# Layer 3 of a graph network: 30 blocks by count matrices instead of 29, own rows on VectorE, the shared row split once, dense products spread to the last fetches

## The chip, the cores and the metric

The kernel runs on one core of a Trainium2 chip. The time is device microseconds (us) of one execution. The kernel before took 2103.5 us, the median of three runs (2099.63 to 2105.44).

## The reference

Three graph-convolution layers over 6250 nodes and 100000 edges, a residual and a layer norm. The edges arrive sorted by destination.

```
src, dst = edges + one loop per node;  deg = count of dst;  dinv = 1/sqrt(deg)
h = x                                              # 6250 x 256
for W, b in ((W1, b1), (W2, b2), (W3, b3)):        # widths 512, 512, 256
    h = relu(segment_sum((h @ W)[src] * dinv[src] * dinv[dst], dst) + b)
out = layernorm(x + h)
```

## The kernel before

**Blocks and tables.** The 6250 nodes are 50 blocks of Q = 125. Each layer has a table in DRAM, one row per node, already multiplied by dinv of its source; the aggregation of a block sums the rows of all sources of its edges, adds the block's own rows (the loops), and multiplies by dinv of the destination. In layer 3 the product with W3 has been taken before (in the work that closes layer 2's blocks), so layer 3 is aggregation, bias, relu, residual and layer norm alone. Every fp32 value is split into a high part and a rest (both float32r, a faster format of TensorE), side by side in 512 columns: `parts` holds so the split rows of all nodes in SBUF, and one 512-column product sums both halves.

**Two ways to aggregate a block.** *Gathered:* GpSimd fetches 128 rows of the table at a time by an indirect DMA (`gather`, L1172); ScalarE casts the high half (L1232), VectorE subtracts for the rest (L1235), and TensorE multiplies by a 0/1 matrix that says to which of the 125 destinations a row belongs (L1200). Such a fetch is a *chunk*; a block has KF = 16. Edges beyond 2048 of a block share one more fetch per ten blocks, the *shared row tile*; in layer 3 it isn't split, so its product is a plain fp32 one (half as many columns, recorded as two matmuls). The 0/1 matrices are made four at a time by VectorE (`more_hots`, L1123), when the first of four is needed. The block's own rows come in by a product with the identity, first in its sum (L1185). *Dense:* a 125 x 6250 matrix of uint8 counts says how often each node is a source; five 125x125 pieces at a time are converted to float32r by ScalarE, every fourth by VectorE (L1132), and 50 products of such a piece with `parts` make the block's sum (L1269). The loops are added into the count matrix (L813).

**Who does what.** `MANY` = 29 blocks (0 to 28) of layer 3 are dense and 21 gathered. Their count matrices are made before: 26 in layer 1, and the others in layer 2, at chunks 50 + gap x n with gap = (612 - 100) // (MANY - 26) = 170. Making one takes 25 bf16 products (L862), 15 comparisons on VectorE (L787), 13 copies out of PSUM on ScalarE (L821), one addition (L813), and a store to DRAM on SP's queue. Layer 2 itself has 38 gathered blocks (608 chunks) and 12 dense ones that TensorE works on beside them.

**Order.** Inside `layer` the instructions of all engines are put out by hand in one loop over chunks (L1217): gather chunk c, cast chunk c-3, subtract chunk c-4, products of chunk c-lag (lag = 9 in layer 3), then the steps of the work that closes finished blocks (`after3`), then dense products until `done` reaches begun + (c + 1 - first) x 50 / spacing (L1249). 45 dense products of block 0 have been done before (`begun`). For layer 3 spacing = (339 - 14) / (29 - 0.9), 339 being the chunks of 21 blocks and three shared tiles; from the last chunk on all dense products that are left are put out at once (L1252). Each engine runs its own list in order and waits on semaphores.

**Closing a block** (`after3`, L1432): load its rows of x on SP's queue (two buffers), sum x dinv + bias and the second half (L1438, L1439), relu and add x (L1444), statistics (L1447, L1449), square root on ScalarE (L1451), reciprocal and scaling (L1454, L1455), store on ScalarE's queue.

Of the kernel before, what the change touches and what calls it, by code (L numbers as in the profile page):

```python
# [10 lines left out]
F32 = mybir.dt.float32  # L11
# [5 lines left out]
ALU = mybir.AluOpType  # L17
# [9 lines left out]
Q = 125  # L27
# [7 lines left out]
HOTS = 4  # L35
# [3 lines left out]
LOANED = 4  # L39
RETURN = 6  # L40
SHORT = 5


COPIED = 3
# [6 lines left out]
BOTH_FROM = 26  # L51
# [4 lines left out]
SPLIT = ((3, 4, BOTH_LAG), (1, 2, 8), (3, 4, 9))  # L56
# [1 line left out]
TEAM = 3  # L58
TEAMS = 4
HOME = 19  # L60
MANY = 29
ALONE = 2
G = 5
GB = Q // G
# [333 lines left out]
def sorted_path(ctx: ExitStack, tc: tile.TileContext, x, edges, starts, found, wts, biases, room, late, out):  # L398
# [14 lines left out]
    nc = tc.nc  # L413
# [4 lines left out]
    N, C = x.shape  # L418
    HID = w1_sb.shape[2]
    EC = d.shape[1]  # L420
    NB = N // Q
# [11 lines left out]
    parts = all_parts[:Q]  # L433
# [3 lines left out]
    dinv = const.tile([Q, NB], F32, name="sdinv")  # L437
# [301 lines left out]
    work = ctx.enter_context(tc.tile_pool(name="swork", bufs=2))  # L739
# [12 lines left out]
    split = split_rows_of(one, "sfirst_split", 0, C)  # L752
# [251 lines left out]
    begun = 0  # L1004
# [36 lines left out]
    def layer(i, width, gathered, dense, after, rows, first=0, spacing=1.0, extras=(), filler=None):  # L1041
# [19 lines left out]
        total = len(items)  # L1061
# [53 lines left out]
        hots = []  # L1115
# [21 lines left out]
        hi_lag, lo_lag, lag = SPLIT[i]  # L1137
# [9 lines left out]
        acc = own_product = None  # L1147

        of_ten, to_split = {}, {}
        ten_halves = split.popleft() if i == 1 else None  # L1150
        shared, rows = rows[:2], rows[2:]

        def gather(c):
            nonlocal turn
            n, b, j = items[c]
            table = both_halves if of_both(c) else tables[i]
            if (i, b, j) == (0, BOTH_FROM, BOTH_LAG + 1):
                hot_stores.appendleft(late_hot_room)
            if b is None:
                row, at = split.popleft() if of_both(c) else shared[n % 2], rest[:, n, 0:1]  # L1160
                of_ten[n] = row
                if i == 1:
                    to_split[c + SPLIT[i][2] + 1] = n
            elif of_both(c):
                row, at = split.popleft(), src[:, b, j:j + 1]
                split_rows[c] = row
            else:
                row, at = rows[turn % len(rows)], src[:, b, j:j + 1]
                assert i > 0 or b < TAIL_FROM or len(hot_stores) == 2
                (landed if halved(c) else split_rows)[c] = row  # L1170
                turn += 1
            nc.gpsimd.indirect_dma_start(out=row, out_offset=None, in_=table,  # L1172
                                         in_offset=bass.IndirectOffsetOnAxis(ap=at, axis=0))

        def product(c):
            nonlocal acc, own_product
            n, b, j = items[c]
            if b is None:
                return
            if j == 0:  # L1180
                acc = sum_bank("acc", 2 if i == 1 else 3)
                own_product = i == 2 or i == 0 and b < BOTH_FROM
                if own_product:

                    nc.tensor.matmul(acc[:Q], lhsT=ident_r[:Q, :Q], rhs=parts[:, b], start=True, stop=False)  # L1185
            if i == 1 and j == KF - LATE:
                by_rows(nc.sync, own_row, tables[1][b * Q:(b + 1) * Q, :])
            several = [(j, split_rows.pop(c))]
            if j == KF - 1:
                several.append((KF, of_ten[b // GRP]))  # L1190
            for k, row in several:
                at = n * (KF + 1) + k
                if at % HOTS == 0:
                    more_hots()
                hot = hots[at // HOTS][:, at % HOTS]
                if row.dtype != F32R:
                    hot = hot.bitcast(F32)
                size = min(row.shape[1], HID)
                for c0 in range(0, row.shape[1], size):
                    nc.tensor.matmul(acc[:Q, :size], lhsT=hot, rhs=row[:, c0:c0 + size], start=(not own_product and k == c0 == 0),  # L1200
                                     stop=(k == KF and c0 + size == row.shape[1]))
            halves = several[0][1]
            if i == 1 and halves in loaned:
                on_loan.remove(halves)
            if halves.dtype == F32R and (returning is None or halves not in loaned):
                split.append(halves)
            if j == KF - 1:
                if i == 1:
                    nc.scalar.activation(own_row, own_row, AF.Copy, scale=dinv[:, b:b + 1])
                ended(now, b, acc)  # L1210
# [3 lines left out]
        with tc.manual_schedule():  # L1214
            more_hots()
            to_sum = 0
            for chunk in range(total + (SHORT if i == 1 else lag)):  # L1217
                now = chunk
                if i == 1:
                    lag = SPLIT[i][2] if returning is None else max(SHORT, SPLIT[i][2] - (chunk - returning) // 2)  # L1220
                if i == 0:
                    lag = TAIL_LAG if TAIL_FROM * KF <= chunk - total + NB * KF < (NB - 1) * KF else BOTH_LAG
# [26 lines left out]
                until = min(len(dense) * NB, begun + int((chunk + 1 - first) * NB / spacing))  # L1249
                if i == 0:  # L1250
                    until = min(until, done + 3)
                if chunk >= total - 1:  # L1252
                    until = len(dense) * NB
                while done < until:
                    m, k = divmod(done, NB)
# [176 lines left out]
    def after3(b, acc, bank):  # L1432
        yield from take("y", 2)
        x_rows.reverse()
        xr = x_rows[0]
        by_rows(nc.sync, xr, x[b * Q:(b + 1) * Q, :])
        y = work.tile([Q, HID], F32, name="szs")[:, :C]
        nc.vector.scalar_tensor_tensor(y, acc[:Q, :C], dinv[:, b:b + 1], b3_sb[:Q], op0=ALU.mult, op1=ALU.add)  # L1438
        nc.vector.scalar_tensor_tensor(y, acc[:Q, C:], dinv[:, b:b + 1], y, op0=ALU.mult, op1=ALU.add)  # L1439
        free(bank, acc)  # L1440
        yield LATE
        r_o = work.tile([Q, HID], F32, name="st")
        r, o = r_o[:, :C], r_o[:, C:]
        nc.vector.scalar_tensor_tensor(r, y, 0.0, xr, op0=ALU.max, op1=ALU.add)  # L1444
        yield 1
        stats = small.tile([Q, nc.vector.BN_STATS_DIM], F32, name="sstats")
        nc.vector.bn_stats(stats, r)  # L1447
        mv = small.tile([Q, nc.vector.BN_AGGR_DIM], F32, name="smv")
        nc.vector.bn_aggr(mv, stats)  # L1449
        sd = small.tile([Q, 1], F32, name="ssd")  # L1450
        nc.scalar.activation(sd, mv[:, 1:2], AF.Sqrt, bias=eps[:Q])  # L1451
        yield SOON
        rs = small.tile([Q, 1], F32, name="srs")
        nc.vector.reciprocal(rs, sd)  # L1454
        nc.vector.tensor_scalar(o, r, mv[:, 0:1], rs, op0=ALU.subtract, op1=ALU.mult)  # L1455
        free("y")
        by_rows(nc.scalar, o, out[b * Q:(b + 1) * Q, :], store=True)
# [12 lines left out]
    def steps(b):  # L1470

        return (NB - b) * KF + NG - b // GRP
# [13 lines left out]
    spacing = 15.0  # L1486
# [26 lines left out]
    nc.sync.dma_start(out=b3_sb, in_=bass.AP(tensor=b3.tensor, offset=b3.offset, ap=[[0, P], [1, C]]))  # L1513
    pieces = ctx.enter_context(tc.tile_pool(name="slate_pieces", bufs=6))
    split = split_rows_of(ctx, "ssplit", 2, C)
    spacing = (steps(MANY) - 14) / (MANY - begun / NB)
    layer(2, C, every[MANY:], many, after3, last_rows, 4, spacing)


# [179 lines left out]
```

## Time and profile before

| | |
|---|---|
| median of three runs | 2103.5 us |
| profiled execution | 2099.5 us, its span 2097.8 us |
| TensorE clock granted, mean | 0.961 |
| layer 2's first gather, layer 3's first gather | 708.5 us, 1646.5 us |
| layer 3's last gather, end | 2084.4 us, 2097.8 us |
| busy in the span | PE 93%, DVE 74%, ACT 64%, POOL 68% |

PE is TensorE's matmuls, PEld its weight loads, DVE VectorE, ACT ScalarE, POOL GpSimd, SP the sync engine; a q behind a name is that engine's instruction queue issuing transfers. The slices cut the span in 40 equal parts, each digit a busy share in tenths. In a group of instructions stand line, engine, operation, what is written and read with the shape, the count, then busy us and mean ns of one, then the idle time just before them and who ended it. Matmuls are pipelined and overlap in the record, so busy time of PE says that something was on it, not how fast it went.

### The profile page before, as it was taken

The page shows a single profiled execution, that of the slowest core. Times are in us where ns is not written, and L with a number is a line of the kernel's source. Part 1 is how long each engine was busy: PE and PEld are TensorE (multiplying, and loading weights), DVE is VectorE, ACT ScalarE, POOL GpSimd, SP SyncE. Part 2 cuts the span into 40 slices and gives each one's busy share as a digit, 9 for nine tenths or more (in the row PEclk, how much of TensorE's full clock was granted, in tenths as well). Part 3 has the DMA queues.
Part 4 walks back from the last instruction along what each step waited for, and adds up shares of the span by engine and source line. Part 5 has one row for each costly group of instructions (what it writes and reads, how often), then busy time and mean ns, then how long its engine had stood idle before and what let it go on. Part 6 is the DMA issues. An engine that isn't in the chain of part 4 may idle for free.

```text
span 2097.8 us, 30169 instructions
## 1 busy us (share of the span) xinstructions
PE 1944.3 (93%) x8687; PEld 1513.0 (72%) x8687; DVE 1555.1 (74%) x2933; ACT 1351.9 (64%) x2584; POOL 1432.8 (68%) x1442
## 2 busy tenths in 40 slices
PE   3489999999998979999999999999998899999996
PEld 2367777777775656788778877887777688888874
DVE  5866778787777668877787777778786377777777
ACT  1566777777776667777776766667665456555553
POOL 2456766777676477767776677577776477777775
PEclk6599999999998989999999999999999999999998
DMA  7877999999999899989998999899978376767674
GB/s 167 260 241 209 256 242 249 248 254 256 250 258 301 229 294 255 264 251 283 290 257 244 279 284 269 236 250 299 267 234 229 99 188 175 192 177 195 172 191 116
DMA packets 235407, 493.47 MB, mean 235 GB/s; under 512 B 43633, under 2 KB 85965, under 8 KB 235231
## 3 DMA queue, kind: packets, MB, share of 16 engines
q0 software_dynamic: 122112, 311.41, 54.3%
q1 hardware_dynamic: 97279, 168.19, 29.1%
q10 hardware_dynamic: 15840, 11.86, 2.3%
q8 instruction: 70, 1.15, 0.2%
q14 instruction: 106, 0.87, 0.1%
HBM read 423.84 MB, written 67.46 MB: 234 GB/s over the span
## 4 chain that ended last, share of the span: by engine, by line
PE 61%; DMA 17%; issue 8%; POOL 6%; DVE 4%; ACT 2%; ACTq 1%; SPq 0%; POOLq 0%; DVEq 0%
DMA room<-tab,ssrc 13%; PE sacc L1200 11%; PE mat_ps L1269 7%; PE smm L1269 6%; POOL room L1172 6%; PE win_ps L1269 6%; PE win_ps L1385 5%; PE sacc L1269 5%; PE str L1269 2%; PE win_ps L1405 2%; PE sacc L1322 2%; PE mat_ps L970 2%; PE sacc L970 2%; PE smm L970 2%; PE win_ps L1200 1%
## 5 line engine op out<-in xcount | busy, mean ns | idle before, releaser
L1172 POOL DMA_INDIRECT room<-tab,ssrc x1040 | 1069.2, 1028 | 398.4 <-issue 168.5
L1235 DVE TENSOR_TENSOR halves<-room,halves 128x512 fp32r<-128x512 f32 (+1 forms) x778 | 427.1, 562 | 242.3 <-ACT halves L1232 233.4
L1232 ACT CAST halves<-room 128x512 fp32r<-128x512 f32 (+1 forms) x778 | 388.9, 517 | 229.9 <-DMA room<-tab,ssrc 175.3
L1200 PE MATMUL sacc<-halves,shot 128*125 128x512 f32 x1384 | 479.4, 411 | 15.4 <-DVE shot L1123 6.6
L1172 POOL DMA_INDIRECT halves<-both,ssrc x352 | 331.0, 940 | 143.6 <-issue 36.8
L1132 ACT CAST piece<-room 125x625 fp32r<-125x625 uint8 x416 | 294.5, 717 | 84.1 <-DVE halves L1235 27.3
L787 DVE TENSOR_TENSOR room<-near_cols,slots 128x625 bf16<-128x625 f32 (+2 forms) x390 | 294.2, 801 | 44.9 <-PE sacc L862 21.3
L1200 PEld LDWEIGHTS sacc<-halves,shot 128*125 128x125 f32 x1384 | 257.3, 190 | 89.5 <-issue 9.4
L1123 DVE TENSOR_TENSOR shot<-near_cols,sdlo 128x500 fp32r<-128x500 f32 x371 | 247.4, 667 | 6.2 <-PE smm L1200 3.7
L1385 PE MATMUL win_ps<-room,w_sb 128*128 128x250 f32 (+1 forms) x832 | 189.9, 372 | 9.3 <-DVE st L1418 4.3
L1269 PE MATMUL mat_ps<-parts,piece 125*125 125x512 f32 x650 | 188.1, 406 | 0.0
L1385 PEld LDWEIGHTS win_ps<-room,w_sb 128*128 128x128 f32 x832 | 154.4, 192 | 36.3 <-DVE st L1418 6.2
L1269 PE MATMUL win_ps<-parts,piece 125*125 125x512 f32 x600 | 172.5, 409 | 5.5 <-ACT piece L1132 5.5
L1269 PE MATMUL smm<-parts,piece 125*125 125x512 f32 x605 | 172.7, 404 | 0.6 <-DVE piece L1132 0.6
L1235 DVE TENSOR_TENSOR parts<-room,parts 128x512 fp32r<-128x512 f32 x198 | 134.2, 689 | 46.8 <-ACT parts L1232 43.6
L932 DVE TENSOR_TENSOR parts<-parts 125x512 fp32r<-125x512 f32 x200 | 137.8, 689 | 30.3 <-ACT parts L930 29.8
L970 PE MATMUL sacc<-parts 125*125 125x512 f32 x400 | 141.8, 427 | 18.0 <-ACT parts L930 10.4
L1232 ACT CAST parts<-room 128x512 fp32r<-128x512 f32 x198 | 120.1, 622 | 52.5 <-DMA room<-tab,ssrc 37.1
L862 PEld LDWEIGHTS <-room 128*125 128x125 bf16 x650 | 89.8, 140 | 76.8 <-issue 30.6
L821 ACT CAST room<-sacc 125x500 uint8<-125x500 f32 (+1 forms) x152 | 105.7, 705 | 60.7 <-PE sacc L862 59.0
L1269 PE MATMUL sacc<-parts,piece 125*125 125x512 f32 x450 | 143.1, 425 | 1.6 <-ACT piece L1132 1.6
L970 PE MATMUL mat_ps<-parts 125*125 125x512 f32 x400 | 137.3, 425 | 0.3 <-DVE st L1327 0.2
(311 smaller groups left out, 3146.4 us busy)
## 6 DMA issues: line engine op xcount, KB each, us to landing
parts<-tab SPq DMA_DIRECT2D x105, 448.0 KB
kept<-room SPq DMA_DIRECT2D x29, 683.6 KB
room<-kept SPq DMA_DIRECT2D x29, 683.6 KB
room<-tab,ssrc POOLq DMA_INDIRECT x1040
tab<-st SPq DMA_DIRECT2D x62, 224.0 KB
both<-parts SPq DMA_DIRECT2D x10, 1120.0 KB
own_row<-tab SPq DMA_DIRECT2D x38, 224.0 KB
parts<-kept SPq DMA_DIRECT2D x60, 136.7 KB
```

The costliest lines, as they stand in the source:

```text
L787: nc.vector.tensor_tensor(out, near_cols[:, :shape[2]].unsqueeze(1).to_broadcast(shape), numbers.unsqueeze(2).to_broadcast(shape), op=ALU. ...
L821: nc.scalar.copy(place[:, :, u * G:(u + len(ms)) * G].rearrange("p k (t r) -> p t k r", r=G), counted_in.rearrange("p (t v) -> p t v", t=2 ...
L932: nc.vector.tensor_sub(to[:, HID:], row, to[:, :HID].bitcast(F32))
L970: nc.tensor.matmul(team_banks[n][:Q], lhsT=team_pieces[(g * CUTS + k // PIECE) % 2][n][:, k % PIECE, :], rhs=both_parts[u % 3][:, h * HID: ...
L1123: nc.vector.tensor_tensor(hot[:, :n], near_cols[:, :Q].unsqueeze(1).to_broadcast([P, n, Q]), dlo.rearrange("p b j -> p (b j)")[:, at:at + ...
L1132: convert(piece, made_or_read[:, c * PIECE:(c + 1) * PIECE, :])
L1172: nc.gpsimd.indirect_dma_start(out=row, out_offset=None, in_=table, in_offset=bass.IndirectOffsetOnAxis(ap=at, axis=0))
L1200: nc.tensor.matmul(acc[:Q, :size], lhsT=hot, rhs=row[:, c0:c0 + size], start=(not own_product and k == c0 == 0), stop=(k == KF and c0 + si ...
L1232: nc.scalar.copy(halves[:, :width], landed[chunk - hi_lag])
L1235: nc.vector.tensor_sub(halves[:, width:], landed.pop(chunk - lo_lag), halves[:, :width].bitcast(F32))
L1269: nc.tensor.matmul(acc_d[:Q], lhsT=got[done // PIECE][:, k % PIECE, :], rhs=parts[:, k], start=(k == 0), stop=(k == NB - 1))
L1385: nc.tensor.matmul(h_ps[:, f, :], lhsT=w2_sb[:, k, (f2 + f) * P:(f2 + f + 1) * P], rhs=zt2[:, k, :wide], start=(k == 0), stop=(k == KH - 1))
```

## The change

Five edits, all for layer 3 (i = 2) but the first, which also adds a matrix to layer 2's work. `MANY` goes from 29 to 30. The shared tile is split once for its ten blocks, into a tile of its own, as layer 2 does it. Own rows of a gathered block are added by VectorE in `after3`, out of `parts`. The next four 0/1 matrices are made as soon as the last product with the previous four has been put out. The lag falls from 9 to 6 over the last chunks (`AT_END`), the spacing is (322 + 1) / (30 - 0.9), and what dense products are left is put out only five chunks after the last gather.

```diff
+END = 1
+AT_END = 6
...
-MANY = 29
+MANY = 30
...
-        ten_halves = split.popleft() if i == 1 else None
+        ten_halves = split.popleft() if i > 0 else None
...
-                if i == 1:
+                if i > 0:
                     to_split[c + SPLIT[i][2] + 1] = n
...
-                own_product = i == 2 or i == 0 and b < BOTH_FROM
+                own_product = i == 0 and b < BOTH_FROM
...
-                if at % HOTS == 0:
+                if at // HOTS == len(hots):
                     more_hots()
...
+            if i == 2 and (at + 1) % HOTS == 0:
+                more_hots()
...
-            for chunk in range(total + (SHORT if i == 1 else lag)):
+            for chunk in range(total + (lag, SHORT, AT_END)[i]):
                 now = chunk
+                if i == 2:
+                    lag = max(AT_END, SPLIT[i][2] - max(0, chunk - total + 2 * AT_END) // 2)
...
-                if chunk >= total - 1:
+                if chunk >= (total + AT_END - 2 if i == 2 else total - 1):
                     until = len(dense) * NB
...
-        y = work.tile([Q, HID], F32, name="szs")[:, :C]
-        nc.vector.scalar_tensor_tensor(y, acc[:Q, :C], dinv[:, b:b + 1], b3_sb[:Q], op0=ALU.mult, op1=ALU.add)
-        nc.vector.scalar_tensor_tensor(y, acc[:Q, C:], dinv[:, b:b + 1], y, op0=ALU.mult, op1=ALU.add)
+        z = work.tile([Q, HID], F32, name="szs")
+        y, lower = z[:, :C], acc[:Q, C:]
+        if b < MANY:
+            nc.vector.scalar_tensor_tensor(y, acc[:Q, :C], dinv[:, b:b + 1], b3_sb[:Q], op0=ALU.mult, op1=ALU.add)
+        else:
+            nc.vector.tensor_tensor(z, acc[:Q], parts[:, b].bitcast(F32), op=ALU.add)
+            nc.vector.scalar_tensor_tensor(y, y, dinv[:, b:b + 1], b3_sb[:Q], op0=ALU.mult, op1=ALU.add)
+            lower = z[:, C:]
+        nc.vector.scalar_tensor_tensor(y, lower, dinv[:, b:b + 1], y, op0=ALU.mult, op1=ALU.add)
...
-    spacing = (steps(MANY) - 14) / (MANY - begun / NB)
+    spacing = (steps(MANY) + END) / (MANY - begun / NB)
     layer(2, C, every[MANY:], many, after3, last_rows, 4, spacing)
```

## Prediction

> **What bounds the kernel now.** The page comes first: engine totals, then the slices. In the slices TensorE is the engine at 9 almost throughout, and its digit falls only in the last one.
>
> ```profile
> PE 1944.3 (93%) x8687; PEld 1513.0 (72%) x8687; DVE 1555.1 (74%) x2933; ACT 1351.9 (64%) x2584; POOL 1432.8 (68%) x1442
> PE   3489999999998979999999999999998899999996
> ```
>
> Layer 3 runs from 1646 us to the end at 2097.8. The table of busy time by stage shows how it is spent:
>
> ```profile
> 1646.00:1700.00 54.00, 48.08 (x195) 37.75 (x194) 30.91 (x78) 28.18 (x62) 41.04 (x42) 0.94 0.58 153
> 1700.00:1750.00 50.00, 50.00 (x217) 40.03 (x216) 36.25 (x97) 29.09 (x68) 38.12 (x40) 1.00 0.69 186
> 2000.00:2050.00 50.00, 49.71 (x214) 39.47 (x213) 38.08 (x103) 29.78 (x71) 38.42 (x39) 1.00 0.67 178
> 2050.00:2098.00 48.00, 31.10 (x114) 21.34 (x112) 33.21 (x91) 17.38 (x45) 27.08 (x28) 0.82 0.39 113
> ```
>
> (Columns: stretch, length, busy us of PE, PEld, DVE, ACT, POOL, then clock, DMA share, GB/s.) TensorE is full until 2050 and then does 114 products in 48 us, where the stretches before did 217 in 50. That last stretch is where this change acts. The groups of layer 3, by shape, give what each engine has to do in it:
>
> ```profile
> L1172 POOL DMA_INDIRECT room<-tab,ssrc x336 | 333.0, 991 | 102.4 <-issue 32.3 <-DVE halves L1235 25.6 <-DVE piece L1132 7.3
> L1269 PE MATMUL win_ps<-parts,piece 125*125 125x512 f32 x500 | 139.9, 404 | 5.5 <-ACT piece L1132 5.5
> L1200 PE MATMUL sacc<-halves,shot 128*125 128x512 f32 x336 | 134.3, 405 | 8.7 <-DVE shot L1123 5.5 <-DVE srs L1454 1.8 <-DVE halves L1235 1.4
> L1269 PE MATMUL smm<-parts,piece 125*125 125x512 f32 x455 | 125.0, 397 | 0.6 <-DVE piece L1132 0.6
> L1269 PE MATMUL mat_ps<-parts,piece 125*125 125x512 f32 x450 | 123.6, 397 | 0.0
> L1200 PE MATMUL sacc<-room,shot 128*125 128x256 f32 x42 | 12.9, 390 | 0.0
> L1185 PE MATMUL sacc<-parts,ident_r 125*125 125x512 f32 x21 | 8.5, 403 | 0.0
> ```
>
> Dense products are 500+455+450 = 1405, products of gathered rows 336, halves of the shared row's fp32 product 42, own-row products 21. Each lasts about 0.4 us, but they overlap, so I need the distance of two starts. The order of time gives it, and the two ends of the layer:
>
> ```profile
> 1646.47 0.95 POOL L1172 DMA_INDIRECT room<-tab,rest  x1 [26.58 <-DMA tab<-st]
> 1654.64 7.54 PE L1269 MATMUL win_ps<-parts,piece 125*125 125x512 f32 x20 [5.27 <-ACT piece L1132]
> 2061.99 1.33 PE L1269 MATMUL win_ps<-parts,piece 125*125 125x512 f32 x5
> 2072.16 0.86 PE L1200 MATMUL sacc<-halves,shot 128*125 128x512 f32 x3
> 2072.86 0.59 PE L1200 MATMUL sacc<-room,shot 128*125 128x256 f32 x2
> 2081.47 2.29 PE L1200 MATMUL sacc<-halves,shot 128*125 128x512 f32 x4 [2.23 <-DVE shot L1123]
> 2084.36 0.95 POOL L1172 DMA_INDIRECT room<-tab,ssrc  x1 [0.30 <-DVE halves L1235]
> 2089.81 0.48 DVE L1438 SCALAR_TENSOR_TENSOR szs<-sacc,sdinv,sb 125x256 f32<-125x256 f32 x1 [1.54 <-PE sacc L1200]
> 2092.95 0.78 ACTq L75 DMA_DIRECT2D out<-st  x2
> ```
>
> Five products in 1.33 us, the last of them 0.4 long: (1.33-0.40)/4 = **0.232 us from start to start**. A half of the shared row's fp32 product: 0.59-0.39 = 0.20; I take 0.215, between that and 0.232. GpSimd issues 339 gathers from 1646.47 to 2084.36: 437.9/338 = **1.296 us a gather**, never waiting longer than 0.3 us:
>
> ```profile
> POOL room L1172 <- issue: 32.9, 108, 0.3
> ```
>
> So two engines are full side by side until 2072: TensorE by the products that the spacing puts between gathers, and GpSimd by issuing. At 2072.16 the dense products are done while eleven gathers are still to be issued, and TensorE then waits for each row. The products left at 2072.16 are those of block 49 and the last three of block 48: some 17 of gathered rows, two shared pairs, one own row, 17 x 0.232 + 4 x 0.215 + 0.23 = 5.0 us of work. They end at 2089.8. **TensorE loses 2089.8 - 2077.2 = 12.6 us there.** Then 8.0 us of the last block's normalisation and store follow to 2097.8.
>
> **The change part by part.** (a) *One block from gathered to dense.* 16 gathers and one shared gather go (block 29 no longer opens a group), 339 to 322. 16 products go, 50 dense ones come. Last gather issued: 1646.5 + 321 x 1.296 = 2062.4, instead of 2084.4.
>
> (b) *Shared row split once.* 42 fp32 halves go (9.0 us); 20 single products of 0.232 come (4.6 us). ScalarE and VectorE get two 128x256 operations each, while 16 casts and subtractions of that size go with block 29's rows. The second split writes the tile that block 39's last product reads; ScalarE meets it two chunks later in the order, so a wait there is short, behind it stand row casts, and TensorE has up to four converted pieces (20 products, 4.6 us) in hand. Nothing is charged.
>
> (c) *Own rows by VectorE.* 21 products go from TensorE (4.9 us), 20 additions of 125x512 out of PSUM come to VectorE. Layer 1 has that very operation:
>
> ```profile
> L1304 DVE TENSOR_TENSOR szs<-sacc,parts x9: 678/690/692, 284.2 to 698.0; 125x512 f32<-125x512 f32 x9
> ...
> L1235 DVE TENSOR_TENSOR halves<-room,halves 128x256 fp32r<-128x256 f32 x336 | 136.2, 418 | 110.3 <-ACT halves L1232 109.8
> ```
>
> The first row is one operation's median in ns (690), the second the groups' mean of one subtraction (418). 20 x 0.69 = 13.8 us on an engine that is busy 36 to 38 of 50 us; block 29's 16 subtractions of 0.42 (6.7 us) go at the same time. VectorE stays near three quarters, so the additions lie in its idle time; without that cover they cost up to 13.8.
>
> TensorE's work in layer 3: 50 x 0.232 = 11.6 added, 16 x 0.232 = 3.7, 9.0 - 4.6 = 4.4 and 4.9 removed: **1.4 us less**. The totals are nearly equal; what changes is where the idle time goes.
>
> (d) *Spacing and lag.* Dense products now run 4.5 a chunk to chunk 326 of 328, so there is always one to do between the last rows; the lag of product behind gather falls from 9 to 6 over the last chunks. TensorE per chunk: (1455+340)/322 x 0.232 = 1.293 us, against 1.296 for a gather. TensorE's end is then the full-queue end, 2077.2 - 1.4 = 2075.8. The last row is issued at 2062.4; a row needs from issue to product what the chain of waits shows at the end,
>
> ```profile
> 2084.36 2.77 DMA room<-tab,ssrc
> ```
>
> 2.77 and then a cast and a subtraction, ready at 2088.1, 3.8 us after its issue. That is 2066.2: 9.6 us ahead of TensorE. So TensorE ends the layer: **2089.8 - 2075.8 = 14.0 us earlier**. Comparison matrices (L1123) are now made one product early; waits on them such as the 2.23 us at 2081.47 should go. I credit none of it in the full stretch.
>
> (e) *The end.* Block 49 and dense block 29 finish within half a us of each other. In VectorE's order all of block 29's seven operations stand ahead of block 49's last ones. One block takes from 2089.81 to 2092.95, 3.1 us, some 2.6 of it VectorE. Block 29 starts about 0.5 us before; and the own-row addition is 0.7: 2.6 - 0.5 + 0.7 = **2.8 us longer** than the 8.0 now. (Between 0.7, if they interleave without loss, and 3.3.) The x rows of both are on time: SP loads them as soon as one of two buffers is free, and for the last blocks of before it did so from 2058 on, before their last products:
>
> ```profile
> 2058.34 16.88 SPq L77 DMA_DIRECT2D room<-in_x  x8
> ```
>
> (f) *One more count matrix in layer 2.* 25 count products, 15 comparisons on VectorE, 13 copies on ScalarE, one store and later its load on SP's queue (a whole count matrix, as for the 29 before). The four late matrices start 128 chunks apart, where three did at 170.
>
> ```profile
> L787 DVE TENSOR_TENSOR hot_pair<-near_cols,slots 128x625 bf16<-128x625 f32 (+2 forms) x36 | 27.8, 801 | 0.7 <-PE str L862 0.5
> ...
> 951.00:1047.00 96.00, 95.16 (x426) 77.66 (x425) 74.27 (x119) 68.78 (x125) 74.18 (x71) 1.00 1.02 286
> 1060.00:1185.00 125.00, 123.88 (x574) 101.42 (x573) 98.02 (x162) 90.87 (x172) 88.47 (x83) 1.00 0.93 259
> 1185.00:1299.00 114.00, 108.31 (x482) 86.55 (x481) 87.67 (x140) 78.37 (x146) 82.17 (x81) 1.00 1.03 281
> 1313.00:1438.00 125.00, 123.92 (x573) 101.33 (x572) 96.38 (x158) 88.95 (x168) 85.37 (x81) 1.00 0.93 255
> 1317.59 0.27 PE L862 MATMUL str<-hot_pair 128*125 128x250 bf16 x1
> 1317.70 0.59 PE L1385 MATMUL win_ps<-room,w_sb 128*128 128x250 f32 x2
> ```
>
> Three late matrices took 36 of these comparisons after 850 us, 0.8 us each, so a new one brings VectorE 12 us. The second and fourth stretch hold a count matrix, the others none. With one, a gather (last x column) takes 125/83 = 1.51 and 125/81 = 1.54 us, without one 1.35 and 1.41. But the count stretches also hold more products per gather (574/83 = 6.9 against 6.0), because the team's blocks finish in them, and TensorE is full: 574 products in 125 us is 0.218 each. So I charge TensorE's time alone: the next product starts 0.11 us behind a count product, 25 x 0.11 = **2.8 us**. Bounds: 0 (the matrix falls into a stretch with idle time) and 15.7, the largest difference of pace, (1.543-1.352) x 82 chunks.
>
> Sum: -14.0 + 2.8 + 2.8 = **-8.4 us**. The profiled execution took 2099.5 us around its span of 2097.8; the median of the runs is 2103.5. I subtract from the median: **2095.1**.
>
> **A rule of the skill.** The stretches show PEld at 40 of 50 us where PE is at 50. The Trainium skill, Perfetto Trace Analysis, "Identifying the Most-Contended Engine", says that matmul busy time is a bad measure and LDWEIGHTS busy share a good one: by it TensorE has a fifth to spare. The Trainium skill, TensorE: Matmul & The Clock Gate, "Wait — 56ns, not 53.3ns?", gives 215.7 ns for a warm 512-column product; at that (an estimate from the page) the 1795 products would need 387 us and not 416. The trace has 0.232 at a clock of 1.00 in group after group, and that is what I go by.
>
> **Rivals.**
> 1. *TensorE isn't the bound; it keeps up with whatever GpSimd issues.* Then the end follows the last gather: 2062.4 + 5.4 (2084.36 to 2089.8) = 2067.8, 8.0 us before 2075.8: -16.4, **2087**. For it: GpSimd is as full as TensorE. Against: products stand 0.232 apart without gaps. 8%.
> 2. *The last rows are late at lag 6.* Six chunks are 7.8 us, 3.8 are needed; VectorE, with the additions and two closing blocks, would have to add 4. Then TensorE stops for a row with dense products queued behind it, and some 5 us of the 12.6 come back: **2100**. For it: the old tail shows exactly such waits. Against: the margin of 9.6 us. 12%.
> 3. *Slower: the count matrix is paid by the pace of its stretch.* Comparisons of 0.8 us on VectorE delay subtractions, rows come free late, gathers late. At 15.7 us: -8.4 + 12.9 = +4.5, **2108**. It decides from 11.2 us upwards. For it: the pace above. Against: the extra products explain the pace. 14%.
>
> **How the numbers follow.** The forecast has 66%, with a range of its own of 2089 to 2101 (tail 0.7 to 3.3, matrix 0 to 6, waits on comparisons gone or not). Rivals 1 and 3 lie at the edges, so the range is 2086 to 2107. About 0.3%, 6.3 us, is what a measurement of this kernel can tell from no change (the three runs spread by 5.8). Faster: four fifths of the forecast and rival 1, 0.6; within: the rest of the forecast, rival 2 and most of rival 3, 0.34; slower: 0.06.
>
> **What would show it.** Right: TensorE at 9 to the last slice; the last dense and the last gathered product within 1 us of each other; the last gather some 8 us or more before them; layer 3 from first gather to last product about 429 us instead of 443; layer 2 longer by 2 to 4. Wrong: products of gathered rows that wait for VectorE or ScalarE in the last 20 us; a first gather of layer 3 later by over 8 us; or products closer than 0.23.

## The result, and the profile after

The changed kernel takes **2129.73 us** (median of 6 runs, 2123.05 to 2135.28) against 2103.81 for the kernel before on the same chip (6 runs, 2094.49 to 2106.19): ratio **1.0139, 95% interval 1.0116 to 1.0162**, slower (the two medians alone divide to 1.0123, 25.9 us). The forecast was 2095.1, faster; the time lies outside its range.

The profiled execution took 2124.5 us, its span 2122.8. The two lines of the page that answer to the first two shown of before:

```profile
PE 1942.2 (91%) x8703; PEld 1509.0 (71%) x8703; DVE 1573.8 (74%) x2953; ACT 1362.4 (64%) x2590; POOL 1418.5 (67%) x1425
PE   3499999999997879999999999989988899999997
```

TensorE has as much to do as before, in 25 us more. Behind the first three, besides the slices that were low before too (13, 15, 31 and 32), slices 14, 27 and 30 fell; the last two lie in layer 2, where only a count matrix was to be added. The last slice went from 6 to 7.

The profiled executions are divided at gathers. One of these places needs a word: the table above the prediction calls 708.5 us layer 2's first gather, but that is layer 1's last one; layer 2's 612 gathers start at 728.2 us, after an idle stretch. The lengths called "layer 2" from here on run from layer 1's last gather, in every run, and so hold some 20 us between the layers (19.7 in before, 19.9 in after); the differences are hardly touched by it.

| us | before | after | difference |
|---|---|---|---|
| layer 1, first gather to its last | 632.4 | 630.5 | -1.9 |
| layer 2, layer 1's last gather to layer 3's first | 938.0 | 972.8 | **+34.8** |
| layer 3, first gather to the end | 451.3 | 442.4 | **-8.9** |

Two executions of one kernel differ by up to 3 us in layer 2 and in layer 3 (e1 and e16, e6 and e18 below), and by up to 6 in layer 1. Layer 3 came near what was forecast (-11.2 = -14.0 + 2.8), layer 2 lost four times that. The table by stage and the order of time of layer 3 after (columns as in the prediction):

```profile
2000.00:2050.00 50.00, 50.00 (x216) 39.92 (x216) 40.06 (x104) 29.65 (x70) 38.42 (x39) 1.00 0.71 187
2050.00:2100.00 50.00, 48.20 (x206) 37.74 (x205) 41.60 (x110) 28.09 (x66) 37.03 (x37) 1.00 0.64 174
2100.00:2123.00 23.00, 11.72 (x51) 9.03 (x49) 10.80 (x30) 4.69 (x13) 0.00 (x0) 0.81 0.11 28
```

```profile
2097.05 0.95 POOL L1174 DMA_INDIRECT room<-tab,ssrc  x1 [0.30 <-DVE smv L1461]
2109.93 1.32 PE L1275 MATMUL mat_ps<-parts,piece 125*125 125x512 f32 x5
2111.09 0.64 PE L1202 MATMUL sacc<-halves,shot 128*125 128x512 f32 x2
2111.29 0.48 DVE L1446 SCALAR_TENSOR_TENSOR szs<-mat_ps,sdinv,sb 125x256 f32<-125x256 f32 x1 [4.90 <-PE mat_ps L1275]
2117.76 0.78 ACTq L77 DMA_DIRECT2D out<-st  x2
```

The last dense and the last gathered product lie 0.5 us apart, and the last gather is issued 14 us ahead of them: the picture that the prediction drew. Then the group of L1200 (now L1202), on the page of before and on that of after:

```profile
L1200 PE MATMUL sacc<-halves,shot 128*125 128x512 f32 x1384 | 479.4, 411 | 15.4 <-DVE shot L1123 6.6
```

```profile
L1202 PE MATMUL sacc<-halves,shot 128*125 128x512 f32 x1388 | 482.0, 412 | 60.7 <-DVE shot L1125 55.1
```

The idle time ahead of these products went from 15.4 to 60.7 us, and nearly all of the rise is put down to `shot`, the 0/1 matrices. Where it is, the waits of TensorE in layer 2 of after (from 850 to 1674 us) tell; the columns are us in all, how many, and the longest:

```profile
PE sacc L1202 <- DVE shot L1125: 41.0, 31, 5.3
PE win_ps L1371 <- ACT room L1402: 3.8, 5, 1.1
```

31 waits, the longest 5.3 us. In the same stage of before, 850 to 1640, the longest line and the one for `shot` are:

```profile
PE sacc L1290 <- DVE szs L1341: 4.7, 3, 3.2
PE sacc L1200 <- DVE shot L1123: 0.2, 1, 0.2
```

Over the whole kernel, and for all gathered rows, this line goes from 6.6 us in before to 68.1 in after (the group above holds only the rows in `halves`):

```profile
PE sacc L1200 <- DVE shot L1123: 6.6, 6, 2.5
```

```profile
PE sacc L1202 <- DVE shot L1125: 68.1, 54, 5.3
```

**The mechanism.** In both versions there is one more call of `more_hots()`, ahead of the loop over chunks (L1215, now L1219). I had overlooked it, and the text above the prediction says so wrongly ("when the first of four is needed"). With `at % HOTS == 0` the call at product 0 is already the second one: group 1 is made when group 0 is first used, so the matrices run a whole group, four products, ahead. With `at // HOTS == len(hots)` the call at product 0 falls away, because one group is there; group 1 is made only when product 4 asks for it. The line that makes it earlier stands under `i == 2` alone. So layers 1 and 2 lost a lead of four products, and layer 3 went from four products to one (to none for one group in seventeen, which begins at a block's shared row: the added line looks only at the last product put out). Layer 1 shows no loss by it (-1.9). The longest of the waits, in order of time, with VectorE's and ScalarE's rows that bear on it (others are left out):

```profile
1417.37 0.69 DVE L1241 TENSOR_TENSOR halves<-room,halves 128x512 fp32r<-128x512 f32 x1 [2.23 <-ACT halves L1238]
1419.76 0.62 ACT L1238 CAST parts<-room 128x512 fp32r<-128x512 f32 x1 [1.81 <-DMA room<-tab,ssrc]
1420.41 0.76 DVE L1241 TENSOR_TENSOR parts<-room,parts 128x512 fp32r<-128x512 f32 x1 [2.35 <-ACT parts L1238]
1422.23 0.69 DVE L1241 TENSOR_TENSOR parts<-room,parts 128x512 fp32r<-128x512 f32 x1 [1.05 <-ACT parts L1238]
1422.84 0.67 DVE L1125 TENSOR_TENSOR shot<-near_cols,sdlo 128x500 fp32r<-128x500 f32 x1
1423.56 1.22 PE L1202 MATMUL sacc<-halves,shot 128*125 128x512 f32 x2 [5.32 <-DVE shot L1125]
```

The comparison needs no gathered row and takes 0.67 us, yet in VectorE's list it stands behind the subtractions of rows that belong to later chunks (layer 2 subtracts two chunks behind the gather and multiplies up to eight behind it). Those wait for ScalarE, and ScalarE waits for a transfer (1.81). TensorE's product, whose own row was long split, waits for all of that: 5.32 us. In before the comparison stands in the same list, four products earlier; there such a delay is met by nobody (0.2 us).

### The profile page after: what moved, and what is told of

It is laid out like the page before. It is cut to its first block, busy times and chain, and to the rows that moved or that the text cites. A ratio compares the mean times of both kernels' runs of the same rounds, so it can differ in the third digit from the quotient of the medians.

```text
span 2122.8 us, 30261 instructions
## 1 busy us (share of the span) xinstructions
PE 1942.2 (91%) x8703; PEld 1509.0 (71%) x8703; DVE 1573.8 (74%) x2953; ACT 1362.4 (64%) x2590; POOL 1418.5 (67%) x1425
## 4 chain that ended last, share of the span: by engine, by line
PE 32%; DMA 5%; issue 4%; DVE 4%; ACT 2%; POOL 2%; SPq 1%; ACTq 0%; DVEq 0%; POOLq 0%
PE sacc L1202 8%; PE win_ps L1275 5%; PE mat_ps L1275 4%; PE win_ps L1391 4%; PE smm L1275 4%; DMA room<-tab,ssrc 3%; PE win_ps L1411 2%; POOL room L1174 2%; DMA own_row<-tab 1%; PE smm L972 1%; PE mat_ps L972 1%; PE sacc L972 1%; DVE halves L1241 1%; DVE shot L1125 1%; ACT halves L1238 1%
## 5 line engine op out<-in xcount | busy, mean ns | idle before, releaser
L1174 POOL DMA_INDIRECT room<-tab,ssrc x1024 | 1056.9, 1032 | 423.4 <-issue 157.9
L1241 DVE TENSOR_TENSOR halves<-room,halves 128x512 fp32r<-128x512 f32 (+1 forms) x762 | 421.0, 564 | 214.9 <-ACT halves L1238 207.3
L1202 PE MATMUL sacc<-halves,shot 128*125 128x512 f32 x1388 | 482.0, 412 | 60.7 <-DVE shot L1125 55.1
L1238 ACT CAST halves<-room 128x512 fp32r<-128x512 f32 (+1 forms) x762 | 382.5, 520 | 184.0 <-DMA room<-tab,ssrc 106.3
L1134 ACT CAST piece<-room 125x625 fp32r<-125x625 uint8 x423 | 299.7, 717 | 104.6 <-PE mat_ps L1275 25.1
L1202 PEld LDWEIGHTS sacc<-halves,shot 128*125 128x125 f32 x1388 | 253.6, 189 | 142.8 <-DVE shot L1125 59.5
L1275 PE MATMUL mat_ps<-parts,piece 125*125 125x512 f32 x700 | 199.8, 404 | 0.0
L1275 PEld LDWEIGHTS mat_ps<-parts,piece 125*125 125x125 f32 x700 | 125.9, 187 | 30.0 <-issue 2.3
L1202 PE MATMUL sacc<-parts,shot 128*125 128x512 f32 x396 | 131.1, 412 | 13.5 <-DVE shot L1125 13.1
```

Source lines behind the costliest of these rows:

```text
L1134: convert(piece, made_or_read[:, c * PIECE:(c + 1) * PIECE, :])
L1238: nc.scalar.copy(halves[:, :width], landed[chunk - hi_lag])
L1241: nc.vector.tensor_sub(halves[:, width:], landed.pop(chunk - lo_lag), halves[:, :width].bitcast(F32))
L1275: nc.tensor.matmul(acc_d[:Q], lhsT=got[done // PIECE][:, k % PIECE, :], rhs=parts[:, k], start=(k == 0), stop=(k == NB - 1))
```

## The experiments

Unless told otherwise they are compared with runs of before on the same chip, and "layer 2" and "layer 3" are the stages of the table above, from one profiled execution each. One thing is needed to read them: e9, e11 and c0 fell on a chip where the kernel before itself takes 2357 us, e12 to e15 on one where it takes 2333 us; their times are set only beside runs of that same chip, and times in us that were expected for them do not apply there.

### The 0/1 matrices: e1, e2, e3

e1 is the changed kernel with the old condition, and without the two added lines:

```diff
-                if at // HOTS == len(hots):
+                if at % HOTS == 0:
...
-            if i == 2 and (at + 1) % HOTS == 0:
-                more_hots()
```

> The changed kernel with one line put back: a group of four 0/1 matrices is made at every fourth product again (the first call before the loop then keeps the groups four products ahead), and the extra call of layer 3 goes. Theory A (the lost lookahead of four products is the whole loss): layer 2, first gather to first gather of layer 3, back from 973 us to 938 + 3 = 941, waits of TensorE for 0/1 matrices from about 41 us back to under 10, layer 3 about 440, time 2092 to 2099, ratio to before 0.995 to 0.998. Theory B (my rival 3: the 30th count matrix and the closer spacing of the late ones slow layer 2): layer 2 stays at 965 to 975, time 2120 to 2130.

Measured: 2099.81 us, ratio **0.9974** (0.9957 to 0.9990); again on another chip, as e16 below, 0.9987 (0.9964 to 1.0009). Layer 2 952.1 instead of 972.8. TensorE's only line for `shot`:

```profile
PE sacc L1202 <- DVE shot L1125: 1.7, 4, 0.7
```

e2 is the opposite: the kernel before with nothing but the new condition.

```diff
-                if at % HOTS == 0:
+                if at // HOTS == len(hots):
```

> The kernel before with that one line changed alone (a group is made when its first product asks for it), 29 matrices, old tail. Theory A: layer 2 grows by 30 us or more with no matrix added, layer 3 some us longer too because it has no early call here, time 2130 to 2145. Theory B: no change, 2100 to 2108.

Measured: 2136.87 us, ratio **1.0146** (1.0125 to 1.0166). Layer 2 971.0 (before 938.0), layer 3 459.1 (451.3), since here no line makes up for it in layer 3. TensorE's waits:

```profile
PE sacc L1200 <- DVE shot L1123: 76.7, 55, 6.5
```

So the condition alone costs 31 us, and taking it back out of the changed kernel gives 0.0165 of the time, 35 us (30 by the medians, which come from different chips): this is shown, from both sides.

e3 asks how much lead is needed: the changed kernel with its "one product early" in all layers.

```diff
-            if i == 2 and (at + 1) % HOTS == 0:
+            if (at + 1) % HOTS == 0:
```

> The changed kernel with the call after every fourth product in all three layers and not in layer 3 alone: lookahead one product. Theory A: the loss in layer 2 depends on how far ahead the group is made; one product of layer 2 is about 1.4 us of a chunk, against 0.67 us for the group plus what stands before it on VectorE, the longest wait being 5.7 us, so about half of the 35 us comes back: layer 2 at 950 to 960, time 2105 to 2118. Theory B: 2120 to 2130.

Measured: 2103.44 us, ratio 0.9994 (0.9970 to 1.0018), better than expected. Layer 2 949.7, as in e1. Over the whole kernel the waits fall to half only, from 68.1 us:

```profile
PE sacc L1202 <- DVE shot L1125: 36.1, 35, 3.0
```

One product of lead gives back nearly all. It also shows that a sum of waits isn't time lost: 36 us of waits here, next to none in e1, and layer 2 is the same; in the whole time e3 is 0.002 above e1, within the intervals. The longest single wait is 3.0 us here against 5.3 in after and 6.5 in e2; that the long ones are what counts fits this, but no run tests it.

### The 30th count matrix: e4, e5, e6, e9, e12, e14, e15

e4 is the kernel before, with a 30th count matrix made and stored in layer 2 and never read; unused work is added, nothing is left out.

```diff
-    kept = dram.tile([MANY, Q, NB * Q], U8, name="kept")
+    kept = dram.tile([MANY + 1, Q, NB * Q], U8, name="kept")
...
-    gap = (steps(TEAM * TEAMS) - 100) // (MANY - FEW - EXTRA)
+    gap = (steps(TEAM * TEAMS) - 100) // (MANY + 1 - FEW - EXTRA)
...
-          + [(50 + gap * n, counts([b], (made,))) for n, b in enumerate(many[FEW + EXTRA:])]
+          + [(50 + gap * n, counts([b], (made,))) for n, b in enumerate(every[FEW + EXTRA:MANY + 1])]
```

> The kernel before with a 30th count matrix made and stored in layer 2 (late ones 128 chunks apart instead of 170) and never read; all else as before. It leaves nothing out and adds unused work. Theory A: 25 x 0.11 = 2.8 us, time 2104 to 2109. Theory B: 12 to 35 us more, time 2115 to 2138.

Measured: 2111.35 us, ratio 1.0029 (1.0008 to 1.0050), 6 us; 2.8 us would be 1.0013, inside the interval. In the profile layer 2 is 949.9, 12 longer. Its two stretches from 1510 to 1530 us, while and just after the DMA engines are full, and then those of before:

```profile
1510.00:1520.00 10.00, 4.25 (x13) 1.98 (x12) 7.61 (x13) 5.36 (x10) 7.56 (x9) 0.74 1.06 289
1520.00:1530.00 10.00, 9.96 (x38) 7.93 (x39) 8.17 (x14) 7.45 (x15) 5.85 (x6) 0.74 0.98 295
```

```profile
1510.00:1520.00 10.00, 7.81 (x28) 4.84 (x27) 7.32 (x12) 6.31 (x11) 7.56 (x9) 1.00 1.04 298
1520.00:1530.00 10.00, 7.90 (x27) 6.59 (x28) 9.94 (x18) 8.18 (x15) 7.56 (x9) 0.66 0.91 286
```

In e4 the fourth store was issued at 1489 us, just ahead, and TensorE did 13 products from 1510 to 1520 instead of 28. The first stretch alone flatters the effect: in the second e4 does more than before, and over both TensorE is busy 14.2 us against 15.7. It made a theory all the same: the store's place is the cost (C), against the matrix's own work (W). e5 and e6 move the starts of the late matrices in e1, so that the last store leaves earlier (1441 us) or later (1551):

```diff
-    gap = (steps(TEAM * TEAMS) - 100) // (MANY - FEW - EXTRA)
+    gap = 115
```

```diff
-    gap = (steps(TEAM * TEAMS) - 100) // (MANY - FEW - EXTRA)
+    starts_at = (50, 190, 330, 478)
...
-          + [(50 + gap * n, counts([b], (made,))) for n, b in enumerate(many[FEW + EXTRA:])]
+          + [(starts_at[n], counts([b], (made,))) for n, b in enumerate(many[FEW + EXTRA:])]
```

> The lookahead kernel (changed, group made at every fourth product) with the four late count matrices 115 chunks apart instead of 128, so the last one is stored some 39 chunks earlier. Theory C (what the 30th matrix costs beyond its products is its store: it goes out at about 1490 us, when the DMA engines are full for 30 us because the teams end and their rows come home, and TensorE falls to half for 10 us): the store is out by about 1440, layer 2 at 940 to 946 instead of 952, time 3 to 9 us under the lookahead kernel, 2091 to 2097. Theory D (it is the work on VectorE and ScalarE, wherever it stands): layer 2 still 949 to 955, time 2098 to 2102.

> The same with the late matrices begun at chunks 50, 190, 330 and 478: the last one is made where no team works any more and stored at about 1560 us, behind the full stretch. Theory C: layer 2 at 938 to 946, time 2090 to 2097. Theory D: some of its VectorE work falls into the stretch where gathers pace the layer, so 950 to 956 and 2099 to 2104.

Measured: e5 2096.42 us, 0.9969 (0.9944 to 0.9994); e6 **2093.46 us, 0.9958 (0.9939 to 0.9977)**, the shortest time of all, below both kernels. Layer 2 is 943.0 and 946.3, against 949.7 to 953.3 in e1, e3, e4, e7, e8 and e16, where the store leaves near 1500. Their intervals overlap with that of e1 (0.9974), so the place is worth 1 to 3 us by the ratios at best. The pair was run once more on one chip, as e16 and e18:

> e6 again (e1 with the late matrices started at chunks 50, 190, 330 and 478), beside e16. If the place of the store matters: 0.001 to 0.003 below e16. If it does not, as e14 suggests: within 0.001 of e16.

Measured: e18 2097.81 us, 0.9977 (0.9955 to 1.0000), e16 2099.29, 0.9987: again 0.001 in the same direction, again within the intervals. Layer 2 of e18 is 949.1, hardly shorter than in the versions with the store near 1500; 953.3 in e16. A stretch where the two profiles differ; e16 first, from 1510 to 1540 us, then e18:

```profile
1510.00:1520.00 10.00, 8.58 (x40) 6.74 (x39) 6.41 (x11) 5.55 (x11) 5.62 (x7) 1.00 1.05 294
1520.00:1530.00 10.00, 5.38 (x18) 2.87 (x16) 7.59 (x12) 5.43 (x10) 7.56 (x8) 0.90 1.07 261
1530.00:1540.00 10.00, 5.39 (x17) 4.15 (x18) 5.87 (x10) 5.45 (x11) 4.52 (x5) 0.67 0.95 302
```

```profile
1510.00:1520.00 10.00, 10.00 (x50) 8.43 (x49) 8.86 (x16) 7.61 (x14) 7.27 (x8) 1.00 1.06 295
1520.00:1530.00 10.00, 7.38 (x29) 4.62 (x27) 8.82 (x14) 7.47 (x14) 7.81 (x8) 0.94 0.96 284
1530.00:1540.00 10.00, 7.90 (x32) 6.61 (x33) 9.98 (x17) 7.96 (x16) 7.63 (x8) 0.72 0.88 258
```

TensorE is busy 25.3 of these 30 us in e18 and 19.4 in e16.

To tell C from W without layer 3's edits, e9 is e4 with the matrix made and not stored, e12 is the same kernel on the other chip, e14 is e4 with the starts of e6, and e15 is before with its three matrices started at 190, 330 and 478:

```diff
-                by_rows(nc.sync, place.rearrange("p k v -> p (k v)"), kept[blocks[n]], store=True)
+                if blocks[n] < MANY:
+                    by_rows(nc.sync, place.rearrange("p k v -> p (k v)"), kept[blocks[n]], store=True)
```

> The kernel before with a 30th count matrix made in layer 2 and neither stored nor read; otherwise as the run in which it is made, stored and not read. It leaves out no part of the computation. Theory C (the store in the full DMA stretch is the cost): of that run's layer 2 of 950 us, 8 to 10 go: 938 to 943, time 2104 to 2108. Theory D (the work of making it): layer 2 at 948 to 952, time 2109 to 2113.

> The kernel before with a 30th count matrix made in layer 2, but neither stored nor read (e9 again, on another chip; unused work is added, nothing is left out). Theory C, the store's place is what costs: 0.9995 to 1.0015 of before, 25 count products and some VectorE time alone. Theory W, the matrix's own work costs: 1.0025 to 1.0035, as e4 with the store.

> e4 (before with an unused 30th count matrix made and stored) with the four late matrices started at chunks 50, 190, 330 and 478, so that the last store leaves near 1551 us and not near 1500. Theory C: 0.9995 to 1.0015. Theory W: 1.0025 to 1.0035, as e4.

> The kernel before with its three late matrices started at chunks 190, 330 and 478 instead of 50, 220 and 390; none is added. Theory C: 0.9995 to 1.0005, since no store of before goes out in the full stretch. If starting the matrices later is a gain as such (for another reason than the store), 0.997 to 0.999.

Measured: e9 2366.53 against 2357.57, 1.0022 (0.9997 to 1.0047); e12 2334.96 against 2333.19, 1.0004 (0.9976 to 1.0032); e14 2342.05, 1.0029 (1.0005 to 1.0053); e15 2335.03, 1.0002 (0.9980 to 1.0025). e14 has the late store (issued at 1699 us; on this chip the stretch with full DMA engines is over at 1640) and the ratio of e4, which speaks against C; e12 without a store has next to nothing, which speaks for the store as such. Layer 2 in the profiles points the same way: 1030.5 in e14 against 1020.1 and 1021.0 in e15 and e13, which make 29 matrices on that chip, but 1006.9 in e12; on the other chip 1034.3 in e9 against 1035.8 and 1036.7 in c0 and e11. But the intervals overlap, each of these lengths is from one execution, and these chips are not those of e4 and e6. **That the 30th matrix costs time is shown (e4, e14). That it costs more than 2.8 us rests on the profiles of layer 2, 949.7 to 953.3 with it against 938.0 and 941.4 without (before and e17); the ratios alone don't tell 6 us from 2.8. Whether the store, its place or the matrix's work is the cause stays open.** Starting matrices later shows no gain as such (e15).

### The new end of layer 3: e7, e8, e11, e13, e16, e17

e7 is e1 with the old end of layer 3: lag 9 throughout, the old spacing, all that is left put out at the last chunk.

```diff
-            for chunk in range(total + (lag, SHORT, AT_END)[i]):
+            for chunk in range(total + (SHORT if i == 1 else lag)):
...
-                if i == 2:
-                    lag = max(AT_END, SPLIT[i][2] - max(0, chunk - total + 2 * AT_END) // 2)
...
-                if chunk >= (total + AT_END - 2 if i == 2 else total - 1):
+                if chunk >= total - 1:
...
-    spacing = (steps(MANY) + END) / (MANY - begun / NB)
+    spacing = (steps(MANY) - 14) / (MANY - begun / NB)
```

> The lookahead kernel with the old end of layer 3: lag 9 throughout, spacing (322 - 14) / 29.1, all that is left put out at the last gather. By my prediction's part (d) the new end keeps TensorE from waiting 12.6 us: then layer 3 goes from 441.5 to about 450 to 454 and the time to 2108 to 2112. The rival: with 30 dense blocks TensorE's own sum (416 us) bounds the layer and GpSimd is ahead of it anyway; dense products at 4.72 a chunk end at chunk 311, some 20 products are left for the tail, and they wait at most 3 us: layer 3 at 440 to 445, time 2098 to 2103.

Measured: 2103.41 us, ratio 1.0005 (0.9985 to 1.0026), 0.003 above e1 and 0.002 above e16, the intervals just overlapping; layer 3 446.5 against 441.5 and 438.9, between the two expectations. e8 is e1 with the own rows of layer 3 by products with the identity again:

```diff
-                own_product = i == 0 and b < BOTH_FROM
+                own_product = i == 2 or i == 0 and b < BOTH_FROM
...
-        if b < MANY:
+        if True:
```

> The lookahead kernel with the own rows of gathered blocks by identity products on TensorE again and not by VectorE. If TensorE bounds layer 3, 20 x 0.232 = 4.6 us come back on it and 0.7 us goes from the last block's closing: layer 3 at 444 to 447, time 3 to 5 us over the lookahead kernel. If VectorE's additions were what holds the layer, it gets shorter: 434 to 440.

Measured: 2099.63 us, ratio 0.9985 (0.9964 to 1.0005); layer 3 441.8 against 441.5 and 438.9, not the 444 to 447 expected. The edit is worth nothing that can be measured, though the 20 products (7.9 us busy) are there again.

e11, e13 and e17 are the same kernel, e1 with 29 blocks (`MANY = 29`); e16 is e1 again, on the chip of e17.

> The lookahead kernel with 29 dense blocks and no 30th matrix: new end of layer 3, own rows by VectorE, shared tile split, old number of blocks. Were TensorE's idle end alone what the change repairs, layer 3 would be as short as with 30, 440 to 443. If GpSimd's 339 gathers at 1.296 us are the bound without the block, the last gather stays 438 us behind the first, and with 5.4 us to the last product and 10 us to the end layer 3 is 448 to 453; layer 2 at 938; time 2098 to 2104.

> e1 with 29 dense blocks in layer 3 instead of 30 (e11 again, on another chip). No fourth late matrix is made and no fourth store goes out in layer 2, so by both theories layer 2 falls back to before's 938 us against e1's 952; layer 3 has 17 gathers more than e1, 22 us by the pace, and 2 us more TensorE work than e1. If layer 3 is bound by TensorE, as the prediction said, the ratio is 0.995 to 0.998; if GpSimd's pace or the rows ending last bind it, 1.000 to 1.006, as e11 gave (1.0055).

> e1 again (the changed kernel with the 0/1 matrices made a whole group ahead), beside e17 and e18. On a chip where the kernel before takes about 2104 us: 0.996 to 0.999, as the first time. On one where it takes 2330 to 2360 us: if the loss of e11 and e13 is that of their 29 blocks, 0.995 to 1.000; if such a chip turns the sign of the whole change, 1.002 to 1.006.

> e1 with 29 dense blocks instead of 30, beside e16. If the 30th block is what layer 3's gain hangs on (TensorE's 2 us less and 17 gathers less), 0.004 to 0.008 above e16. If the loss belongs to the chip, within 0.002 of e16.

Measured: e11 2371.78 against 2357.57, 1.0055 (1.0034 to 1.0076); e13 2344.31 against 2333.19, 1.0042 (1.0025 to 1.0058); e17 2108.51 us, **1.0036** (1.0015 to 1.0056), against e16's 2099.29 us, 0.9987 (0.9964 to 1.0009). So the loss belongs to the 29 blocks and not to a chip. Two stretches of e17, then of e16:

```profile
1850.00:1900.00 50.00, 47.16 (x197) 36.07 (x197) 36.02 (x95) 28.76 (x68) 38.12 (x40) 1.00 0.68 180
2000.00:2050.00 50.00, 46.72 (x199) 36.25 (x198) 37.65 (x98) 26.62 (x64) 38.71 (x38) 1.00 0.70 183
```

```profile
1850.00:1900.00 50.00, 50.00 (x217) 39.99 (x216) 40.16 (x106) 29.18 (x66) 38.14 (x39) 1.00 0.74 190
2000.00:2050.00 50.00, 50.00 (x216) 40.01 (x215) 40.50 (x109) 28.99 (x67) 38.25 (x39) 1.00 0.72 189
```

The gathers are as dense in both (38 to 40 in 50 us). With 29 blocks the new spacing leaves TensorE at 199 products where it could do 217, and the layer ends after its 339th gather. With 30 it is full to the end. Layer 3's length in the four combinations, all with the 0/1 matrices a group ahead (before lacks the other edits too: own rows by VectorE, for which e8 finds no measurable gain with 30 blocks, and the shared row's split, which the other three have):

| | old end | new end |
|---|---|---|
| 29 blocks | 451.3 (before) | 459.7 (e17) |
| 30 blocks | 446.5 (e7) | 438.9, 441.5 (e16, e1) |

With 30 blocks the new end gains 5 to 8 us on top of the 4.8 that they bring with the old one; with 29 blocks layer 3 is 8.4 us longer than in before. Of these 8.4 us, 3.4 stand before the last gather (441.3 us behind the first instead of 437.9), 2.4 between it and the last product, and 2.6 behind that, where two blocks now close together. That they are the new end's doing is argued from the idle TensorE above; own rows and the split shared row were not taken back out with 29 blocks.

c0 is the kernel before itself, unchanged. It was meant to show the spread of a stage between two executions and fell on a chip of the other kind:

> The kernel before once more, for the spread of a stage between two profiled executions: layer 2 at 936 to 940 and layer 3 at 450 to 453 if stages can be compared to 2 us; layer 1 has differed by up to 8 us between kernels that are the same there.

Measured: 2362.57 us, one execution; layer 2 is 1035.8 and layer 3 549.5, so it says nothing on the spread. Its lines are in the last section.

## Why the prediction was wrong, point by point

- **(d), its sentence on the comparison matrices, is the step that failed:** "Comparison matrices (L1123) are now made one product early; waits on them such as the 2.23 us at 2081.47 should go." They are made one product early in layer 3, instead of four, and not early at all in layers 1 and 2. Waits of TensorE on them rose from 6.6 us to 68.1, instead of going. Price: 31 us alone (e2), 35 taken back (e1), where the sum has nothing for it. None of the rivals had it; my list of what each edit does had this one as a matter of layer 3 only. With that line put back, the rest of the change comes out at -5.5 and -2.7 us by the ratios of e1 and e16; -8.4 had been forecast.
- **(d), TensorE's end 14.0 us earlier:** right. From first gather to last product 431.3 us were measured, 429 forecast, 443.3 before; with the matrices a group ahead 430.3 (e1) and 427.9 (e16). The working was right too: full TensorE to the end, the last rows in time. One count in it is a little off: from 2072.16 us on before has 19 products of gathered rows, not some 17, which takes 0.5 us from the 12.6. And e7 and e17 show that this isn't the sum of two gains, as "12.6 + 1.4" reads: with 30 blocks and the old end 437.7 us were measured, with 29 and the new end 449.1.
- **(e), 2.8 us longer at the end:** right; 11.1 us after the last product, 10.8 forecast.
- **(a)** right as a count: 322 gathers, in 416.7 us (1680.4 to 2097.1), 1.298 each against 1.296.
- **(b)** nothing charged: no wait on it shows in layer 3 of after, and it wasn't tried alone.
- **(c)** cost nothing, as said; e8 adds that it gains nothing measurable either, so the 4.9 us less on TensorE do not show in the time.
- **(f), the 30th matrix at 2.8 us:** too small by the profiles, 12 in layer 2 (949.9 against 938.0 in e4, 953.3 against 941.4 in e16 and e17), inside the bounds of 0 to 15.7; by the ratio of e4 6 us, with 2.8 in its interval. Rival 3 had the direction; whether the pace of VectorE is the reason, as it says, stays open. At 6 us -5 is left of layer 3's -11.2, about what e1 has (-5.5).
- **Rivals 1 and 2** fall: TensorE ends last, and no gathered product waits at lag 6.
- **The rule by the weight loads:** the Trainium skill, Perfetto Trace Analysis, "Identifying the Most-Contended Engine", would have given TensorE a fifth of headroom at an LDWEIGHTS share of 40 in 50 us. e16 has 40.0 where products stand as densely as in any stretch (217), e17 36 where TensorE does wait. The share tells the two apart, but here 80% goes with a TensorE that has no idle time left.

Together, from single executions: -8.9 (layer 3) + 12 (the matrix) + 21 (the lead, 972.8 - 952.1 in layer 2) gives 24, against 25 between the two spans.

## What to carry to other kernels

A condition that decides *when* a helper is called is to be read with every call of that helper, those ahead of the loop too: count the lead in products, before and after, in each loop that shares the code. Work that needs no data still comes late if it stands in an in-order list behind work that waits for data, so it is put out early. And two engines that are both nearly full are balanced together: here spreading the work to the end went with a gain once the other engine's count (gathers) had been brought down to match, and with a loss before.

## What the runs showed of the hardware that was not expected

Between chips the kernel before takes 2100 to 2105 us or 2333 and 2357. On such a chip (c0) one instruction lasts as long as elsewhere: a gather 1029 ns against 1028 in before, VectorE's subtractions (L1235, `halves`) 562 in both, ScalarE's casts (L1232) 517 in both; the granted clock of TensorE is 0.941 against 0.961 in the mean. The idle time between the instructions grows. The gathers' group in c0, then some of its waits:

```profile
L1172 POOL DMA_INDIRECT room<-tab,ssrc x1040 | 1070.3, 1029 | 588.2 <-issue 246.3 <-DVE halves L1235 237.9 <-DVE parts L1235 35.7
```

```profile
DVE halves L1235 <- issue: 77.2, 72, 6.4
DVE piece L1132 <- remote: 52.0, 8, 12.9
PE sacc L1200 <- issue: 24.5, 30, 3.2
```

1029 ns each, and idle for 588 us ahead of them; in before, on the chip of the prediction:

```profile
L1172 POOL DMA_INDIRECT room<-tab,ssrc x1040 | 1069.2, 1028 | 398.4 <-issue 168.5 <-DVE halves L1235 93.1 <-DVE parts L1235 30.5
```

"issue" is a wait for nothing that the profile shows, here up to 6.4 us on VectorE; "remote" is a release whose sender it doesn't name. What they are stays open. For a study of 0.3% it means that only runs of one chip can be set side by side.
